# Layer 0 of a chain of attention layers: first-layer points in interleaved pairs, units folded over eight steps, one third-layer call per tile of scores

## The chip, the cores and the metric
The kernel runs on one core of a Trainium2 chip. The metric is the device time of one execution in microseconds (us). Smaller is better. All arithmetic is 32-bit floating point.

## The reference, cut to what matters
The program is a chain of four attention layers on an input of 2 x 512 channels x 32 x 32 pixels. The change lies in the first of them (layer 0), a deformable attention with 8 heads of 64 channels. Each head attends from 1,024 query pixels to 64 sampled key points. To the scores a bias is added that a small perceptron computes from the distance between query and key:

```python
pos = grid_q[:, :, None, :] - grid_kv[:, None, :, :]          # 1024 queries x 64 keys x (x, y)
bias = jnp.sign(pos) * jnp.log1p(jnp.abs(pos))
bias = jax.nn.relu(bias @ cpb_w1 + cpb_b1)                    # 2 -> 128
bias = jax.nn.relu(bias @ cpb_w2 + cpb_b2)                    # 128 -> 128
bias = (bias @ cpb_w3 + cpb_b3)                               # 128 -> 1
sim = jnp.einsum('bhid,bhjd->bhij', qh, kh) + bias
attn = jax.nn.softmax(sim, axis=-1)
```

There are 2 x 8 x 64 = 1,024 key points, and for each of them the perceptron runs on 1,024 queries. An output projection and a residual follow, then the feed-forward part of layer 0 and three further layers of attention, which the change does not touch.

## The kernel before
Layer 0 works through 8 tiles of scores (`NT`); a tile holds two heads, 128 key points by 1,024 queries. A tile has 32 steps (`NR`), each of four points. One long loop (line 892) runs over the 256 steps. The engines execute their instructions in the order in which the program issues them (`in_order`, line 58), so what is written into the loop first also stands first in the queue of each engine.

In each step:

- **First layer** (`first`, line 589, on VectorE). The logarithm of the distance separates into x and y, so a point's first layer is a table of 32 x-values (`tx`) plus a table of 32 y-values (`ty`), added and clipped at zero in one custom instruction (line 599) that writes 128 x 1,024 numbers `h1` (hidden units on the partitions, queries along the row). Four instructions a step, `AHEAD` = 7 points ahead of their use, into a ring of 11 buffers, 8 of them in the weight area `wa`. The tables for 16 points are loaded by SyncE's queue (`load_tabs`, line 573) and scaled by ScalarE (`scale_tab`, line 587) once in four steps.
- **Second layer** (`second`, line 609, on TensorE). The 128 outputs are computed in four parts of 32. For a part, the four points of the step use the four 32-column strips of the array side by side: 8 matmuls in the program, 16 records in the trace, into a PSUM tile `z` (three buffers of two banks). ScalarE applies bias and relu (line 625) into an SBUF tile.
- **Joining** (`joined`, line 630, on VectorE). The third layer's weights were moved into the second layer, up to a sign. Two instructions a step add part 0 to part 1 and part 2 to part 3. GpSimd's DMA then adds the second pair to the first (line 934, 512 KB, a DMA that accumulates in its destination). What is left is a *unit*: 4 points x 32 partial sums on the partitions.
- **Folding** (POOL's queue, accumulating DMAs). A unit's partitions are added in halves: odd onto even (line 927, 256 KB), then every second of those onto the first (128 KB). Four units in a row share one buffer, the *whole*: the first folds in itself (line 929), the other three copy half of what is left into the whole by SyncE (line 931) and add the other half by GpSimd (line 937).
- **Third layer** (`third`, line 635, on TensorE). Every 16 steps, four wholes are summed over their partitions by 8 matmuls with weights of +-1 and 0 into the tile of scores `sim` (one PSUM buffer). It happens 20 steps after the first unit of the 16 was begun (`due = i - 20`, line 899). The second call of a tile is followed by `scores` (line 653), and `sim` is then finished by a generator `behind`, which issues the rest of the tile's work in small pieces, two a step: `finish` (softmax; it holds `pt`, line 668, and `mx`, line 671), `offsets` (the 36 taps of a small convolution, line 408) and `samples` (the sampled keys; `pk` and `pvo`).

The wholes rotate through six buffers (`h2p`: `bridge` 0 to 5) and the other units through four (`h2j`). The last 16 steps (from `LAST`) go by twos in place of fours.

Of the kernel before, what the change touches and what calls it, by code (L numbers as in the profile page):

```python
# [19 lines left out]
P = 128  # L20
# [59 lines left out]
def kernel(ctx: ExitStack, tc: tile.TileContext, a: dict, out: bass.AP):  # L80
# [111 lines left out]
    def layer0(l0, fold_d, t2_b, o2_b):  # L192
# [6 lines left out]
        h2q = l0.enter_context(tc.tile_pool(name="att_h2q", bufs=3))  # L199
        h2p = cycle([bridge[:, k, :] for k in range(6)])  # L200
        h2j = cycle([bridge[:, 6, :], bridge[:, 7, :], *(one.tile([P, HW], F32, name=f"h2j{k}") for k in range(2))])
# [18 lines left out]
        qkw = next(h2j).rearrange("p (j q n) -> p j q n", j=2, q=NPAIR)  # L220
# [15 lines left out]
        ring = [one.tile([P, HW], F32, name=f"h1{k}") for k in range(3)]  # L236
        ring += [qkv2.rearrange("p k n -> p (k n)")[:, k * HW : (k + 1) * HW] for k in range(6)]
        ring += [proj2.rearrange("p k n -> p (k n)")[:, k * HW : (k + 1) * HW] for k in range(2)]
# [13 lines left out]
        ones = one.tile([P, P], F32, name="ones")  # L252
        nc.gpsimd.memset(ones, 1.0)
# [25 lines left out]
        w3_16 = one.tile([P, 48], F32, name="w3_16")  # L279
# [7 lines left out]
        def bias_weights():  # L287
            sort = h2b.tile([P, 7, P], F32, name="sort", tag="h2")
            row, below, w2t = [sort[:, k, :] for k in range(3)]
            perm = sort[:, 3:, :].rearrange("p b (r u) -> p b r u", u=32)  # L290
            few = one.tile([P, 28], F32, name="few")
# [69 lines left out]
            quarter = few[:, 26:28]  # L361
            for k in range(2):
                nc.vector.tensor_reduce(quarter[:, k : k + 1], ident[:, 2 + k : P : 4], AX.X, ALU.add)
                nc.vector.scalar_tensor_tensor(eighth, quarter[:, k : k + 1], 8.0, eighth, ALU.mult, ALU.add)
            nc.vector.tensor_scalar(w3_16[:, 16:32], row[:, 0:16], eighth, 0.0, ALU.add, ALU.is_equal)
            nc.vector.tensor_scalar(w3_16[:, 16:32], w3_16[:, 16:32], w3sign[:, 1:2], None, ALU.mult)
# [118 lines left out]
        def samples(t):  # L485
# [5 lines left out]
            ow = one.tile([P, C], F32, name="ow")  # L491
            nc.sync.dma_start(out=ow, in_=a["out_w"][pr * P : (pr + 1) * P, :])
# [18 lines left out]
            wx = one.tile([P, P], F32, name="wx")  # L511
# [15 lines left out]
            accumulate(pk[:, 1, :], [(wsum[:, 2:3].to_broadcast([P, P]), ident)])  # L527
            yield
            shift = one.tile([P, P], F32, name="shift")
# [12 lines left out]
            kq = one.tile([P, P], F32, name="kq")  # L542
# [3 lines left out]
            values = one.tile([P, P], F32, name="values")  # L546
# [12 lines left out]
        NCH = NR // 4  # L559
        LAST = NT * NR - 16  # L560
        tabs_of = {}

        def load_tabs(c):

            t, rc = divmod(c, NCH)
            assert t in tables
            tabs_of[c] = []
            for ax in range(2):
                src = slog_d[t, ax].rearrange("(q r) i -> q r i", q=4)
                tab = two.tile([P, 16, 32], F32, name=f"tab{ax}")  # L570
                if 4 * c < LAST:
                    q, r = rc % 4, rc // 4 * 16
                    nc.sync.dma_start(out=tab, in_=src[q, r : r + 16, :].partition_broadcast(P))
                else:
                    q, r = rc % 2 * 2, 16 + (rc - 4) // 2 * 8
                    nc.sync.dma_start(
                        out=tab.rearrange("p (q r) i -> p q r i", q=2),
                        in_=src[q : q + 2, r : r + 8, :].partition_broadcast(P),
                    )
                tabs_of[c].append(tab)  # L580

        def scale_tab(c, ax):
            tab, w = tabs_of[c][ax], col("cpb_w1", ax)
            if c == 0:
                nc.vector.tensor_scalar(tab, tab, w, 0.0 if ax else col("cpb_b1"), ALU.mult, ALU.add)
            else:
                nc.scalar.activation(tab, tab, AF.Identity, bias=0.0 if ax else col("cpb_b1"), scale=w)

        def first(p):

            chunk, point = divmod(p, 16)
            if point == 0:
                tabs_of.pop(chunk - 1, None)
                if chunk + 1 < NT * NCH:
                    load_tabs(chunk + 1)
            tx, ty = tabs_of[chunk]
            h1 = ring[p % len(ring)]

            nc.vector._custom_dve(  # L599
                TENSOR_ADD_SAT,  # L600
                out=h1.rearrange("p (y x) -> p y x", x=W),
                in0=tx[:, point, :].unsqueeze(1).to_broadcast([P, H, W]),
                in1=ty[:, point, :].unsqueeze(2).to_broadcast([P, H, W]),
                s0=float(np.finfo(np.float32).max),
                s1=0.0,
            )
            return h1

        def second(i, h1s, part):

            z = zt([P, HW], "z")
            lo = BLOCK[part]
            for half in range(2):
                n = slice(half * HALF, (half + 1) * HALF)
                for point in range(4):
                    nc.tensor.matmul(  # L616
                        z[point * 32 : point * 32 + 32, n],
                        cpb_w2[:, lo : lo + 32],
                        h1s[point][:, n],
                        start=True,  # L620
                        stop=True,
                    )
            ring = h2q if part % 2 else h2b if part else h2j if i % (4 if i < LAST else 2) else h2p
            h2 = ring.tile([P, HW], F32, name="h2", tag="h2") if ring in (h2q, h2b) else next(ring)
            nc.scalar.activation(h2, z, AF.Relu, bias=b2h[:, part : part + 1])  # L625
            return h2
# [8 lines left out]
        def third(sim, r, h2s, fours=(), halves=range(2), wide=False):  # L635

            for half in halves:
                n = slice(half * HALF, (half + 1) * HALF)
                w = w3_16[:, 16 - r : 48 - r] if wide else w3[:, 24 - r : 56 - r]
                ways = [(quad, w, h2) for quad, h2 in enumerate(h2s)]  # L640
                for k in range(2):
                    w = w3_4[:, 28 - r - 4 * k : 60 - r - 4 * k]
                    ways += [(quad, w, pair[k]) for quad, pair in enumerate(fours, len(h2s))]
                for k, (quad, w, h2) in enumerate(ways):
                    nc.tensor.matmul(
                        sim[quad * 32 : quad * 32 + 32, n], w, h2[:, n], start=(r == 0 and k < 4), stop=False
                    )
# [9 lines left out]
        def finish(t, sim):  # L657
# [4 lines left out]
            simb = one.tile([P, HW], F32, name="simb", tag="simb")  # L662
# [11 lines left out]
            at = one.tile([P, 8, P], F32, name="at", tag="simb")  # L674
# [42 lines left out]
        def finish_last(sim, eights, fours, right_sums, left_sums):  # L717
# [7 lines left out]
            simb = one.tile([P, HW], F32, name="simb", tag="simb")  # L725
# [90 lines left out]
        nat = [[next(h2p).rearrange("p (k n) -> p k n", k=2) for _ in range(2)] for _ in range(3)]  # L816
# [68 lines left out]
        h1s, parts, joins, sim, w1s = {}, {}, {}, None, None  # L885
        behind = chain(small_steps, offsets(1), samples(0))
        AHEAD = 7

        for p in range(AHEAD):
            h1s[p] = first(p)  # L890
        late_loads()
        for i in range(steps):
            for k, part in enumerate((1, 0, 3, 2)):
# [3 lines left out]
                if p < 4 * steps:  # L897
                    h1s[p] = first(p)
                due = i - 20
                if k == 1 and 0 <= due < LAST and due % 16 == 0:  # L900
                    t, r = divmod(due, NR)
                    if r == 0:
                        sim = ps_s.tile([P, HW], F32, name="sim")
                    third(sim, r, [joins.pop(due + j) for j in range(0, 16, 4)], wide=True)
                    if r:
# [10 lines left out]
                if LAST <= i - 2 and i < steps - 2:  # L916
# [4 lines left out]
                    if i - 3 >= LAST and i % 2 and k == 3:  # L921
                        nc.gpsimd.dma_start(out=joins[i - 3][1:P:2], in_=joins.pop(i - 2)[1:P:2], accum_op=ALU.add)
                if 0 <= i - 2 < LAST:
                    j = (i - 2) % 4
                    whole, own = joins[i - 2 - j], joins[i - 2]
                    if k == 0:
                        nc.gpsimd.dma_start(out=own[0:P:2], in_=own[1:P:2], accum_op=ALU.add)  # L927
                    if k == 3 and j == 0:
                        nc.gpsimd.dma_start(out=own[0:P:4], in_=own[2:P:4], accum_op=ALU.add)
                    if k == 3 and j:  # L930
                        nc.sync.dma_start(out=whole[j:P:4], in_=own[0:P:4])
                if k == 1 and i - 1 in parts:
                    other = joined(parts.pop(i - 1), 2)
                    nc.gpsimd.dma_start(out=joins[i - 1], in_=other, accum_op=ALU.add)  # L934
                j = (i - 3) % 4
                if k == 1 and 0 <= i - 3 < LAST and j:
                    nc.gpsimd.dma_start(  # L937
                        out=joins[i - 3 - j][j:P:4], in_=joins.pop(i - 3)[2:P:4], accum_op=ALU.add
                    )
# [5 lines left out]
                if k == 1 and due == LAST:  # L945
                    third(sim, 16, [joins.pop(due + j) for j in range(0, 8, 2)])
# [1325 lines left out]
```

## Time and profile before
| | |
|---|---|
| three runs | 3,348.35, 3,349.49, 3,349.53 us; median 3,349.49 |
| profiled execution | 3,353.46 us, span 3,351.7 us |
| mean granted TensorE clock | 0.998 of full speed |
| busy: TensorE, VectorE, ScalarE, GpSimd | 3,323.8, 2,673.0, 1,805.5, 676.7 us |
| first and last `z` matmul | 59.6 and 1,981.6 us |
| GpSimd's DMA queue | 68,400 packets, 231.26 MB |
| HBM read, written | 71.46 MB, 10.83 MB |

The profile names the engines PE (TensorE matmul), PEld (its weight loads), DVE (VectorE), ACT (ScalarE), POOL (GpSimd) and SP (SyncE). A group is named by line, engine, operation, and the tiles that it writes and reads. `wa` and `h` as outputs of line 599 are buffers of the ring `h1`; `bridge` and `h2j` are buffers of units. A wait is put down to what ended it.

### The profile page before, as it was taken

The numbers are of one execution on the slowest core, as the hardware profiler recorded it, in microseconds if no ns is written. First come the engines' busy times: TensorE is split into PE (matmuls) and PEld (weight loads), VectorE is DVE, ScalarE is ACT, GpSimd is POOL, SyncE is SP. The second block draws the span as 40 slices with busy tenths as digits, with TensorE's granted clock in tenths as the row PEclk, the third lists the DMA queues.
The fourth block names the chain that finished last, engine by engine and source line by source line (L and its number), as shares of the span: only waits on it lengthen the run. The fifth ranks groups of instructions, "written<-read, shape, count | busy, mean of one in ns | idle before, by whom it ended". The sixth has DMA issues, their size and how long they took to land.

```text
span 3351.7 us, 61808 instructions
## 1 busy us (share of the span) xinstructions
PE 3323.8 (99%) x24813; PEld 1611.7 (48%) x24813; DVE 2673.0 (80%) x3540; ACT 1805.5 (54%) x2774; POOL 676.7 (20%) x804
## 2 busy tenths in 40 slices
PE   9999999999999999999999999999999999999999
PEld 4333333332333332333333339999953443687777
DVE  6999999999999799999999976455446465665556
ACT  4866877877877577877877652122136245122221
POOL 0333333333333233333333310000000000000000
PEclk9999999999999999999999999999999999999999
DMA  5778787787787577787787751000100000000111
GB/s 166 157 161 166 153 168 156 152 166 153 158 167 155 103 162 155 159 169 152 158 166 157 161 135 58 14 8 14 52 0 14 26 29 20 7 7 3 30 32 36
DMA packets 142488, 343.97 MB, mean 103 GB/s; under 512 B 36464, under 2 KB 51440, under 8 KB 141424
## 3 DMA queue, kind: packets, MB, share of 16 engines
q0 software_dynamic: 68400, 231.26, 36.5%
q1 hardware_dynamic: 72496, 103.95, 10.7%
q8 instruction: 197, 3.23, 0.4%
q10 hardware_dynamic: 1296, 4.72, 0.4%
q14 instruction: 99, 0.81, 0.1%
HBM read 71.46 MB, written 10.83 MB: 25 GB/s over the span
## 4 chain that ended last, share of the span: by engine, by line
PE 82%; DVE 9%; issue 5%; DMA 2%; ACT 1%; POOL 1%; DVEq 0%; SPq 0%; POOLq 0%; ACTq 0%
PE z L616 38%; PE pma L135 6%; PE pw L1435 6%; PE pmb L135 5%; PE pmv L1435 4%; PE score L1614 3%; PE pv L1626 3%; DVE wa L599 3%; PE pm L1435 3%; PE score L1435 3%; PE pmt L1435 1%; PE ppr L1435 1%; DVE h L599 1%; DMA bridge<-h 1%; DVE bridge L630 1%
## 5 line engine op out<-in xcount | busy, mean ns | idle before, releaser
L616 PE MATMUL z<-wa,cpb_w 128*32 128x512 f32 x11904 | 1779.2, 593 | 5.8 <-ACT h L625 3.7
L625 ACT ACTIVATE h<-z,b2h 128x1024 f32<-128x1024 f32 x768 | 851.3, 1114 | 347.9 <-PE z L616 310.6
L616 PE MATMUL z<-h,cpb_w 128*32 128x512 f32 x4480 | 983.2, 593 | 1.6 <-ACT h L625 1.6
L616 PEld LDWEIGHTS z<-wa,cpb_w 128*32 128x32 f32 x11904 | 497.2, 110 | 888.2 <-issue 778.1
L599 DVE CUSTOM_DVE_ANT_1 wa<-tab,tab 128x1024 f32<-128x1024 f32 x744 | 878.1, 1216 | 1.3 <-PE z L616 1.1
L616 PEld LDWEIGHTS z<-h,cpb_w 128*32 128x32 f32 x4480 | 256.6, 110 | 328.6 <-issue 292.1
L599 DVE CUSTOM_DVE_ANT_1 h<-tab,tab 128x1024 f32<-128x1024 f32 x280 | 332.9, 1216 | 2.3 <-PE z L616 2.2
L630 DVE SCALAR_TENSOR_TENSOR h<-h,turn,h 128x1024 f32<-128x1024 f32 x256 | 326.8, 1276 | 4.3 <-ACT h L625 4.3
L625 ACT ACTIVATE bridge<-z,b2h 128x1024 f32<-128x1024 f32 x162 | 180.8, 1116 | 121.4 <-PE z L616 119.0
L927 POOL DMA_DIRECT2D bridge<-bridge x150 | 127.6, 850 | 547.2 <-DMA bridge<-h 510.5
L630 DVE SCALAR_TENSOR_TENSOR bridge<-bridge,turn,h 128x1024 f32<-128x1024 f32 x162 | 206.8, 1277 | 4.2 <-ACT bridge L625 4.2
L934 POOL DMA_DIRECT2D bridge<-h x161 | 163.4, 1015 | 213.2 <-DVE h L630 123.6
L1278 ACT COPY p<-pma 128x128 f32<-128x128 f32 x80 | 21.3, 266 | 334.7 <-PE pma L135 334.7
L1270 DVE TENSOR_TENSOR upper<-pma,p 128x256 f32<-128x256 f32 x80 | 33.7, 422 | 178.6 <-ACT p L1278 178.5
L1615 ACT ACTIVATE p<-score 128x512 f32<-128x512 f32 x256 | 130.0, 624 | 81.2 <-PE score L1614 79.6
L927 POOL DMA_DIRECT2D h2j<-h2j x90 | 76.2, 847 | 323.0 <-DMA h2j<-h 293.6
L1647 DVE TENSOR_TENSOR acc<-acc,p 128x1024 f32<-128x1024 f32 x96 | 111.0, 1217 | 19.4 <-ACT p L1615 19.3
L625 ACT ACTIVATE h2j<-z,b2h 128x1024 f32<-128x1024 f32 x94 | 105.0, 1117 | 37.9 <-PE z L616 37.3
L1614 PE MATMUL score<-q,k 64*128 64x512 f32 x512 | 120.7, 604 | 1.1 <-DVE gm L1191 1.1
L630 DVE SCALAR_TENSOR_TENSOR h2j<-h2j,turn,h 128x1024 f32<-128x1024 f32 x94 | 120.0, 1276 | 0.0
L1626 PE MATMUL pv<-p,vT 128*64 128x512 f32 x512 | 116.5, 598 | 0.0
L937 POOL DMA_DIRECT2D bridge<-h2j x90 | 111.9, 1244 | 2.6 <-issue 1.8
(458 smaller groups left out, 4379.8 us busy)
## 6 DMA issues: line engine op xcount, KB each, us to landing
bridge<-h POOLq DMA_DIRECT2D x161, 512.0 KB, 5.5
h2j<-h POOLq DMA_DIRECT2D x94, 512.0 KB, 5.9
bridge<-bridge POOLq DMA_DIRECT2D x159, 256.0 KB, 3.9
tab<-slog_d SPq DMA_DIRECT2D x128, 256.0 KB, 4.6
h2j<-h2j POOLq DMA_DIRECT2D x90, 256.0 KB, 3.2
bridge<-bridge POOLq DMA_DIRECT2D x150, 128.0 KB, 5.4
bridge<-bridge SPq DMA_DIRECT2D x90, 128.0 KB, 3.7
bridge<-h2j SPq DMA_DIRECT2D x90, 128.0 KB, 3.6
```

The source lines that it names most:

```text
L135: nc.tensor.matmul(pm, w, m, start=(k == 0), stop=(k == len(pairs) - 1))
L599: nc.vector._custom_dve(TENSOR_ADD_SAT, out=h1.rearrange("p (y x) -> p y x", x=W), in0=tx[:, point, :].unsqueeze(1).to_broadcast([P, H, W] ...
L616: nc.tensor.matmul(z[point * 32 : point * 32 + 32, n], cpb_w2[:, lo : lo + 32], h1s[point][:, n], start=True, stop=True,)
L625: nc.scalar.activation(h2, z, AF.Relu, bias=b2h[:, part : part + 1])
L630: nc.vector.scalar_tensor_tensor(h2, h2, turn[:, part // 2 : part // 2 + 1], parts.pop(part + 1), ALU.mult, ALU.add)
L927: nc.gpsimd.dma_start(out=own[0:P:2], in_=own[1:P:2], accum_op=ALU.add)
L934: nc.gpsimd.dma_start(out=joins[i - 1], in_=other, accum_op=ALU.add)
L937: nc.gpsimd.dma_start(out=joins[i - 3 - j][j:P:4], in_=joins.pop(i - 3)[2:P:4], accum_op=ALU.add)
L1435: nc.tensor.matmul(out, stationary(l, k), moving(r, k), start=start and k == 0, stop=k == nk - 1, skip_group_check=not start,)
L1614: nc.tensor.matmul(sc, ks[m][r, s * P : (s + 1) * P], qs[m][r, n], start=True, stop=True)
L1615: nc.scalar.activation(p[:, part], sc, AF.Exp, scale=64 ** -0.5)
L1626: nc.tensor.matmul(pv[half][part * 64 : part * 64 + 64], vt[s % 4][:, lo : lo + 64], lps[s, half][:, part, :], start=(s == 0), stop=(s == 7),)
```

## The change
First layer: two points per instruction. The ring holds six double buffers in which the 32-pixel rows of two points alternate. The table `ty` is written by ScalarE in the order (y, point), as `pairs`, so that (y, point) is one axis; the table loaded for it has one buffer instead of two. `second` reads each point with its rows 64 numbers apart. `AHEAD` is 8.

Folding: in the first seven tiles (`WIDE`) eight units share a whole. Every unit folds twice in itself, and a third time (64 KB) one step later: the first within itself, the others by a copy of 16 partitions and an accumulate of 16 partitions into the whole. The first half of the last tile keeps fours (`shared`), its last 16 steps twos.

Third layer: in the first seven tiles one call per tile with weights `w3_32`, 37 steps after the tile's first unit was begun.

Buffers: units and wholes take their buffers from one list of ten, `room`, in the order in which they come free. Parts 1 and 3 have four buffers instead of three. To make space, `ones` moves into a scratch tile, and `simb`, `at`, `wx`, `shift`, `kq`, `values` and `ow` share buffers with others; `ow` is loaded after `pk`.

```diff
-        h2q = l0.enter_context(tc.tile_pool(name="att_h2q", bufs=3))
-        h2p = cycle([bridge[:, k, :] for k in range(6)])
-        h2j = cycle([bridge[:, 6, :], bridge[:, 7, :], *(one.tile([P, HW], F32, name=f"h2j{k}") for k in range(2))])
+        h2q = l0.enter_context(tc.tile_pool(name="att_h2q", bufs=4))
+        room = deque([bridge[:, 7, :], *(one.tile([P, HW], F32, name=f"h2j{k}") for k in range(2))])
+        room += [bridge[:, k, :] for k in range(7)]
...
-        ring = [one.tile([P, HW], F32, name=f"h1{k}") for k in range(3)]
-        ring += [qkv2.rearrange("p k n -> p (k n)")[:, k * HW : (k + 1) * HW] for k in range(6)]
-        ring += [proj2.rearrange("p k n -> p (k n)")[:, k * HW : (k + 1) * HW] for k in range(2)]
+        ring = [one.tile([P, 2 * HW], F32, name=f"h1{k}") for k in range(2)]
+        ring += [qkv2.rearrange("p k n -> p (k n)")[:, k * 2 * HW : (k + 1) * 2 * HW] for k in range(3)]
+        ring.append(proj2.rearrange("p k n -> p (k n)"))
...
+        WIDE = (NT - 1) * NR
         LAST = NT * NR - 16
+
+        def shared(i):
+            return 8 if i < WIDE else 4 if i < LAST else 2
...
-                tab = two.tile([P, 16, 32], F32, name=f"tab{ax}")
+                tab = (one if ax else two).tile([P, 16, 32], F32, name=f"tab{ax}")
...
             tab, w = tabs_of[c][ax], col("cpb_w1", ax)
+            to = tab
+            if ax:
+                tab = tab.rearrange("p (a k) i -> p a i k", k=2)
+                to = two.tile([P, 8, 32, 2], F32, name="pairs")
+                tabs_of[c][ax] = to
...
-                nc.scalar.activation(tab, tab, AF.Identity, bias=0.0 if ax else col("cpb_b1"), scale=w)
+                nc.scalar.activation(to, tab, AF.Identity, bias=0.0 if ax else col("cpb_b1"), scale=w)
...
-            tx, ty = tabs_of[chunk]
-            h1 = ring[p % len(ring)]
+            tx, ty = tabs_of[chunk][0][:, point : point + 2, :], tabs_of[chunk][1][:, point // 2]
+            h1 = ring[p // 2 % len(ring)].rearrange("p (y k x) -> p y k x", k=2, x=W)
...
-                in0=tx[:, point, :].unsqueeze(1).to_broadcast([P, H, W]),
-                in1=ty[:, point, :].unsqueeze(2).to_broadcast([P, H, W]),
+                in0=tx.unsqueeze(1).to_broadcast([P, H, 2, W]),
+                in1=ty.unsqueeze(3).to_broadcast([P, H, 2, W]),
...
-            return h1
+            return [h1[:, :, k, :] for k in range(2)]
...
-                        h1s[point][:, n],
+                        h1s[point][:, half * 16 : half * 16 + 16, :],
...
-                due = i - 20
-                if k == 1 and 0 <= due < LAST and due % 16 == 0:
-                    t, r = divmod(due, NR)
-                    if r == 0:
-                        sim = ps_s.tile([P, HW], F32, name="sim")
-                    third(sim, r, [joins.pop(due + j) for j in range(0, 16, 4)], wide=True)
-                    if r:
+                for due, n in ((i - 37, 8), (i - 20, 4)):
+                    if k != 1 or not 0 <= due < LAST or due % NR or shared(due) != n:
+                        continue
+                    t = due // NR
+                    sim = ps_s.tile([P, HW], F32, name="sim")
+                    third(sim, 0, [taken(due + j) for j in range(0, 4 * n, n)], wide=w3_32 if n == 8 else w3_16)
+                    if n == 8:
...
                 if 0 <= i - 2 < LAST:
-                    j = (i - 2) % 4
-                    whole, own = joins[i - 2 - j], joins[i - 2]
+                    own, n = joins[i - 2], shared(i - 2)
+                    whole, j = joins[i - 2 - (i - 2) % n], (i - 2) % n
                     if k == 0:
                         nc.gpsimd.dma_start(out=own[0:P:2], in_=own[1:P:2], accum_op=ALU.add)
-                    if k == 3 and j == 0:
+                    if k == 3 and (n == 8 or j == 0):
                         nc.gpsimd.dma_start(out=own[0:P:4], in_=own[2:P:4], accum_op=ALU.add)
-                    if k == 3 and j:
+                    elif k == 3:
                         nc.sync.dma_start(out=whole[j:P:4], in_=own[0:P:4])
+                if k == 2 and 0 <= i - 3 < WIDE:
+                    own, j = joins[i - 3], (i - 3) % 8
+                    if j:
+                        nc.sync.dma_start(out=joins[i - 3 - j][j:P:8], in_=own[0:P:8])
+                    else:
+                        nc.gpsimd.dma_start(out=own[0:P:8], in_=own[4:P:8], accum_op=ALU.add)
...
-                j = (i - 3) % 4
-                if k == 1 and 0 <= i - 3 < LAST and j:
-                    nc.gpsimd.dma_start(
-                        out=joins[i - 3 - j][j:P:4], in_=joins.pop(i - 3)[2:P:4], accum_op=ALU.add
-                    )
+                for at in (i - 4, i - 3):
+                    if k != 1 or at < 0 or at >= LAST or (shared(at) == 8) != (at == i - 4):
+                        continue
+                    n = shared(at)
+                    j = at % n
+                    if j:
+                        own = taken(at)
+                        nc.gpsimd.dma_start(
+                            out=joins[at - j][j:P:n], in_=own[n // 2 : P : n], accum_op=ALU.add
+                        )
```

`taken(i)` removes unit `i` from the live units and puts its buffer at the end of `room`; part 0 of each step takes the buffer at the front.

## The prediction
> **What bounds the kernel now.** I read the page's busy shares and slices first, then the busy time by stretch, the costliest groups, the timelines of weight loads and of VectorE in a quiet stretch, and the waits.
>
> The page: TensorE (PE) 99%, VectorE (DVE) 80%.
> ```profile
> PE 3323.8 (99%) x24813; PEld 1611.7 (48%) x24813; DVE 2673.0 (80%) x3540; ACT 1805.5 (54%) x2774; POOL 676.7 (20%) x804
> DVE  6999999999999799999999976455446465665556
> ```
> The slices show that DVE's 80% is an average of two stages: nearly full until about 2,000 us (layer 0, which the change is in), half empty after. The busy time in four stretches of layer 0's loop says the same in us (columns: PE, PEld, DVE, ACT, POOL, clock, DMA share, GB/s):
> ```profile
> 60.00:500.00 440.00, 437.27 (x3976) 136.99 (x3972) 431.60 (x395) 331.74 (x444) 150.84 (x175) 1.00 0.78 163
> 500.00:1000.00 500.00, 496.57 (x4488) 156.06 (x4484) 487.56 (x445) 374.78 (x514) 175.26 (x204) 1.00 0.78 158
> ```
> PE and DVE are both full, the DMA engines are at 0.78. Two full engines cannot both set the pace, so the groups are asked:
> ```profile
> L616 PE MATMUL z<-wa,cpb_w 128*32 128x512 f32 x11904 | 1779.2, 593 | 5.8 <-ACT h L625 3.7
> L599 DVE CUSTOM_DVE_ANT_1 wa<-tab,tab 128x1024 f32<-128x1024 f32 x744 | 878.1, 1216 | 1.3 <-PE z L616 1.1
> L616 PE MATMUL z<-h,cpb_w 128*32 128x512 f32 x4480 | 983.2, 593 | 1.6 <-ACT h L625 1.6
> L630 DVE SCALAR_TENSOR_TENSOR bridge<-bridge,turn,h 128x1024 f32<-128x1024 f32 x162 | 206.8, 1277 | 4.2 <-ACT bridge L625 4.2
> ```
> The last column is idle time before the group: almost none on either engine. The 593 ns of a z matmul is a modelled end, so the pitch is taken from the weight loads (start, busy, engine, group, idle before):
> ```profile
> 623.38 0.13 PEld L616 LDWEIGHTS z<-wa,cpb_w 128*32 128x32 f32 x4 [0.30 <-issue]
> 623.81 0.13 PEld L616 LDWEIGHTS z<-wa,cpb_w 128*32 128x32 f32 x4 [0.30 <-issue]
> ```
> Four records start together, the next four 0.43 us later (0.4295 as a mean). The rows show 11,904 + 4,480 = 16,384 records, 4,096 fours, 16 in each of the 256 steps: 16 x 0.4295 = 6.87 us of PE a step, 1,759 us in all. From the first z (59.6) to the last (1,981.6) are 1,922 us. I laid all matmul starts of that stretch in order and subtracted each kind's usual pitch: what is left over is 33 us, 20 of it small pauses of about 0.1 us where the kind of matmul changes, and only 13 us in pauses over 0.25 us. **PE is 99% occupied by work that it must do.** DVE against that:
> ```profile
> 1000.81 2.35 DVE L599 CUSTOM_DVE_ANT_1 wa<-tab,tab 128x1024 f32<-128x1024 f32 x2
> 1003.08 1.28 DVE L630 SCALAR_TENSOR_TENSOR h<-h,turn,h 128x1024 f32<-128x1024 f32 x1
> 1004.28 2.35 DVE L599 CUSTOM_DVE_ANT_1 h<-tab,tab 128x1024 f32<-128x1024 f32 x2
> ```
> Two L599 and one L630 take 3.47 us by their starts (1000.81 to 1004.28), so DVE needs 6.93 us a step plus small work. It is a close second. Its waits tell that it is ahead of PE once a tile of 32 steps, when it meets work that comes late in PE's order (60 to 1,985 us; total, times, longest):
> ```profile
> DVE mx L671 <- PE pt L668: 29.4, 7, 5.8
> DVE x L715 <- PE pp L705: 23.1, 4, 7.1
> ```
> That is 52 us in which DVE had nothing to do.
>
> [...] the L599 pair starts 1,134 ns apart[...] The trace's 128 KB accumulates of L929 landed in 3.5 us[...]
>
> **The change part by part.**
> Third layer (PE): one call is 8 matmuls, 16 records, 4 fours: 1.72 us. The first seven tiles make one call instead of two: 7 x 1.72 = 12.0 us, all on PE, which is the path. **-12.0.** The eighth tile keeps its calls.
> First layer (DVE): 1,024 instructions of 1,134 ns become 512 of 2 x 1,067 + 67 = 2,200 ns: 34 us less on DVE, 6.80 a step, now under PE's 6.87. Off the path: 0. It can help only in the 13 us of pauses; I count -1.
> z's moving rows now jump every 32 elements. The trace has one such case, L343 in rows of 32 out of 128: its second pass was followed 0.112 us later by the next matmul, as contiguous ones of 128 columns are (`pk`, 0.112). 0[...].
> `scale_tab` (ScalarE, ACT): 63 of the 126 calls of 760 ns read with a stride. L408, strided, takes 408 ns for 64 elements and L678, contiguous, 313: 1.5 ns per element, so +0.75 us for 512. Once in four steps; in the busiest stretch (the 36 taps) ACT is busy 36.1 of 38.8 us, one or two such calls fit the 2.7 idle, and PE can run on in the other two of three z buffers (3.4 us). 0 to +4; I take +1.
> Folding (POOL and SP): each of the 224 wide steps issues one more GpSimd accumulate (16 rows, 64 KB), and the copy of SP shrinks from 32 rows to 16 but comes in 7 of 8 steps instead of 3 of 4. POOL's own loop: L927 is issued, 0.6 us later L934 (512 KB), whose landing the next L927 waits for.
> ```profile
> POOL bridge L927 <- DMA bridge<-h: 331.2, 94, 7.7
> POOL h2j L927 <- DMA h2j<-h: 200.0, 57, 6.3
> ```
> (of 400 to 1,600 us.) 0.6 + landing + 0.3 comes to 6.4 us, 7.7 in every fourth step where the tables load too, 6.8 as a mean; the step takes 7.50. The extra issue (0.83 to 1.25 us, L929 and L937) goes into the 3.4 us that POOL waits in each step; its data, 16 packets of about 0.29 us over 16 engines, adds 0.3 us of DMA time. The loop becomes about 7.1: still covered, no longer by much. What waits behind POOL: L934's source (3 buffers) and the room of part 0. By the order of the list of free buffers, freed units used to come back after two or three steps, now after three to five in most steps and after two in seven steps of a tile. I take +1, bounds -2 and the rival's price.
> The third call stands two steps behind the last fold, as before; PE's waits for it come to 1.5 us in all. With one stage more: 0.
> Edits with one answer: bias weights get about ten small DVE operations, 0.16 to 0.23 us each, 2 us, hidden in DVE's wait for `pb`:
> ```profile
> DVE o_b L855 <- PE pb L135: 8.0, 1, 8.0
> ```
> If that cover were gone, +2. Shared tags and the later `ow` load (SP waits for `pk`, with the next copies behind it) lie steps ahead of their users: 0. `AHEAD` 8 in pairs: two pairs (4.4 us) from 52.8 are ready at 57.2, before the first z: 0.
> **Sum**: -12.0 - 1 + 1 + 1 = -11. The profiled execution took 3,353.5 (span 3,351.7 and 1.8 around it), so it becomes 3,342.5; it was 4.0 above the median 3,349.5, which becomes **3,338.5**, rounded to 3,338.
>
> **The rivals.**
> (a) Forecast: PE's path, 3,332 to 3,342. Chance 0.57.
> (b) DVE does set the pace, and PE only looks full: for it the chain between 66 and 175 us, which runs through L599 and L630; against it the matmul starts. It would give 34 us, but PE's floor allows only 12 + 13: 3,325. Chance 0.06.
> (c) The saving comes back as waits: the later fold lands late at the third call (1.5 us x 7), or ACT's longer `scale_tab` meets the finish of a tile, which is one step later. 3,343 to 3,354. Chance 0.19.
> (d) Slower: POOL's loop becomes the bound. The extra accumulate doesn't hide, because the 256 KB one lands late (5.5 us in table steps) and the next L927 stands behind. It decides from a mean loop of 7.5 us. With half an issue and the data, 7.7: 224 x 0.2 = +45, 3,394; with a full one, 8.0: +112. For it: the chain at 118 to 162 us goes through POOL and `DMA bridge<-h`, and a pause of 1.8 us on PE follows at 175. Chance 0.12.
> (e) The strided rows slow z, up to 3,405. Chance 0.06. That the change doesn't do what it says is excluded by the instruction lists: 56 third-layer matmuls fewer, 512 L599-type instructions, 224 accumulates more.
>
> **How the numbers follow.** 0.2% (6.7 us) is about what a measurement can tell from no change. Faster: (a) and (b), 0.63; same: (c), 0.19; slower: (d) and (e), 0.18. The range leaves out (b)'s end and most of (d) and (e): 3,328 to 3,358; (a)'s own is 3,332 to 3,342.
>
> **What would show it.** Right: fours of z still 0.43 apart; sim's matmuls fewer, the loop's end 11 us earlier; DVE's share of the loop down from 96% (1,849 of 1,922 us) to about 94%, its waits on PE longer; the first-layer instruction near 2,200 ns by starts. Wrong: ACT's z evictions waiting for DMA, POOL without any wait for DVE (d), a z pitch over 0.43 (e), L599 above 2,300.

## The result, and the profile after

| | before | after |
|---|---|---|
| median, us | 3,349.5 (6 runs, 3,347.9 to 3,352.4) | 3,378.7 (6 runs, 3,375.1 to 3,384.1) |
| profiled span, us | 3,351.7 | 3,378.4 |
| mean granted TensorE clock, profiled execution | 0.998 | 0.997 |
| first and last `z` matmul, us | 59.6 and 1,981.6 | 59.8 and 2,005.1 |

The ratio is 1.009, 95% interval 1.0079 to 1.0100. The change is slower by 29 us, where 11 us faster were forecast. The z matmuls keep their pitch, about 0.43 us from one group of four to the next, so neither the clock nor the strided rows account for the loss (weight loads of the changed kernel):

```profile
623.34 0.13 PEld L635 LDWEIGHTS z<-h,cpb_w 128*32 128x32 f32 x4 [0.30 <-issue]
623.76 0.13 PEld L635 LDWEIGHTS z<-h,cpb_w 128*32 128x32 f32 x4 [0.30 <-issue]
```

The page of the changed kernel, first the busy shares and VectorE's slices:

```profile
PE 3322.3 (98%) x24701; PEld 1601.7 (47%) x24701; DVE 2642.3 (78%) x3039; ACT 1803.6 (53%) x2774; POOL 858.4 (25%) x1027
...
DVE  6998998998998798998998976464446566665656
```

PE has 112 records fewer (7 calls of 16). DVE's row now dips every third slice, once per tile. The stretches of the loop (columns as before):

```profile
60.00:500.00 440.00, 431.87 (x3908) 132.70 (x3900) 420.89 (x272) 328.45 (x438) 190.49 (x224) 1.00 0.84 162
500.00:1000.00 500.00, 491.96 (x4415) 151.89 (x4412) 475.61 (x309) 371.31 (x514) 229.63 (x270) 1.00 0.85 161
```

PE stood still for 8.1 and 8.0 us of them, against 2.7 and 3.4 before, though it had less to do. The waits of PE in the loop (what waits and what ended it; total, times, longest) name the place. The first line is from before, where L645 was the third-layer call; the others are from after:

```profile
PE sim L645 <- DMA bridge<-bridge: 1.5, 2, 1.3
...
PE sim L664 <- DMA bridge<-bridge: 15.6, 5, 3.9
PE z L635 <- ACT h2j L644: 6.1, 3, 3.0
PE sim L664 <- DMA h2j<-h2j: 3.9, 1, 3.9
...
PE sim L664 <- DMA bridge<-h2j: 3.1, 1, 3.1
PE sim L664 <- DMA bridge<-h: 2.9, 1, 2.9
```

L664 is the third-layer call; it waits once in each of the first seven tiles, and at the end of the eighth in `finish_last`. In the line of L635 and `h2j` PE waits for ScalarE's part 0, and ScalarE, by its own waits, for a buffer of `room`, which a late accumulate still reads or fills:

```profile
ACT bridge L644 <- DMA bridge<-bridge: 28.5, 15, 3.7
ACT h2j L644 <- DMA bridge<-h2j: 12.0, 3, 5.8
```

In all ScalarE waits 61 us for DMAs in the loop, which is one of the signs of being wrong that the prediction named; the other, POOL without any wait for DVE, did not appear. The forecast added nothing to the 1.5 us of waits at the third-layer call and +1 for the room of part 0. Repeating the sum of PE's starts over the loop, pauses within the third-layer call come to 28.6 us (2.0 before), pauses between z matmuls to 18.9 (6.9 before): +26.6 and +12.0 against the 12.0 saved. That is the 26.7 us by which the span of the profiled execution grew; 23.4 of them lie before the last z, the rest at the call in `finish_last`.

**One of these waits, read in order.** Around the second tile's call, from the timeline of all engines (start, length, engine and line, idle before):

```profile
326.55 0.85 POOL L951 DMA_DIRECT2D bridge<-bridge  x1 [2.11 <-DMA bridge<-h]
...
327.09 1.22 POOL L964 DMA_DIRECT2D bridge<-h  x1
...
327.66 1.46 POOL L972 DMA_DIRECT2D bridge<-h2j  x1
...
329.94 1.03 PE L664 MATMUL sim<-bridge,w 128*32 128x512 f32 x6
...
330.46 0.84 POOL L953 DMA_DIRECT2D bridge<-bridge  x1 [0.57 <-DMA bridge<-bridge]
...
334.45 0.85 POOL L951 DMA_DIRECT2D bridge<-bridge  x1 [3.16 <-DMA bridge<-h]
...
334.83 1.88 PE L664 MATMUL sim<-bridge,w 128*32 128x512 f32 x10 [3.85 <-DMA bridge<-bridge]
```

POOL issues a unit's 512 KB accumulate (L964) and the last 64 KB one of an older unit (L972), waits for the 256 KB fold to land and issues L953, and waits for the 512 KB to land and issues L951. From one L951 to the next are 7.9 us. PE begins the call at 329.94, is through six records and stands 3.85 us, until this L972, which brings in the tile's last unit, has landed (at 334.48 by its DMA record).

**The loop.** I took the steps in which POOL issued the 512 KB accumulate (L934 before, L964 after) straight after the first fold (L927, L951), so that nothing but landings set its pace, and measured from one first fold to the next. This period, *the loop*, is 0.85 us of issue plus the landing of the 512 KB accumulate ("tables" are steps in which the first layer's tables load, "fold" is the 128 KB one of L929 or L953 beside it):

| | steps | loop without tables, us | with tables and fold, us | mean, us | 512 KB lands after (no tables), us |
|---|---|---|---|---|---|
| before | 105 | 6.59 | 8.13 | 6.86 | 5.74 |
| after | 171 | 7.16 | 8.54 | 7.50 | 6.31 |

PE's step is 6.87 us of z. Before, POOL's loop just kept up. Now it does not. Call *lag* the distance from the start of ScalarE's part 0 to the L964 of the same step, as the median over the tiles for each place in the tile (single steps reach more). The lag, 2 to 5 us before in most steps, grows within each tile to 7 to 8.5 us, and falls to 1 us where PE stands at the call. At the call 7 to 8 of lag, 0.6 of issues ahead and 6 to 7 of landing make some 15 us. The order of the loop leaves two steps, 13.7 us, less the 1.7 that the part's own z matmuls take between the call and ScalarE: 12.0. About 3 are missing, and 2.7 to 4.1 are what PE stood at the seven calls.

The chain that ended last shows it in one line, by engine (before it was 82% PE and 2% DMA), and by line:

```profile
PE 55%; DMA 30%; issue 6%; DVE 5%; POOL 4%; ACT 1%; DVEq 0%; POOLq 0%; SPq 0%; ACTq 0%
DMA bridge<-h 21%; PE z L635 13%; DMA h2j<-h 6%; PE pma L135 6%; PE pw L1470 6%; PE pmb L135 5%; PE pmv L1470 4%; PE score L1649 3%; PE pv L1661 3%; PE pm L1470 3%; PE score L1470 3%; DMA bridge<-bridge 2%; POOL bridge L951 2%; PE ppr L1470 1%; DVE wa L618 1%
```

### The profile page after: what moved, and what is told of

The parts are those of the page before. It is cut to its first block, busy times and chain, and to the rows that moved or that the text cites. A ratio compares the mean times of both kernels' runs of the same rounds, so it can differ in the third digit from the quotient of the medians.

```text
span 3378.4 us, 61170 instructions
## 1 busy us (share of the span) xinstructions
PE 3322.3 (98%) x24701; PEld 1601.7 (47%) x24701; DVE 2642.3 (78%) x3039; ACT 1803.6 (53%) x2774; POOL 858.4 (25%) x1027
## 2 busy tenths in 40 slices
DMA packets 147859, 349.44 MB, mean 103 GB/s; under 512 B 40496, under 2 KB 55472, under 8 KB 146800
## 4 chain that ended last, share of the span: by engine, by line
PE 55%; DMA 30%; issue 6%; DVE 5%; POOL 4%; ACT 1%; DVEq 0%; POOLq 0%; SPq 0%; ACTq 0%
DMA bridge<-h 21%; PE z L635 13%; DMA h2j<-h 6%; PE pma L135 6%; PE pw L1470 6%; PE pmb L135 5%; PE pmv L1470 4%; PE score L1649 3%; PE pv L1661 3%; PE pm L1470 3%; PE score L1470 3%; DMA bridge<-bridge 2%; POOL bridge L951 2%; PE ppr L1470 1%; DVE wa L618 1%
## 5 line engine op out<-in xcount | busy, mean ns | idle before, releaser
L635 PE MATMUL z<-wa,cpb_w 128*32 128x512 f32 x10880 | 1195.2, 593 | 8.6 <-ACT h2j L644 6.1
L618 DVE CUSTOM_DVE_ANT_1 wa<-tab,pairs 128x2048 f32<-128x2048 f32 x340 | 776.4, 2284 | 5.0 <-PE z L635 4.7
L635 PEld LDWEIGHTS z<-wa,cpb_w 128*32 128x32 f32 x10880 | 346.2, 110 | 819.1 <-issue 707.5
L635 PE MATMUL z<-h,cpb_w 128*32 128x512 f32 x5504 | 609.4, 593 | 3.2 <-ACT h L644 1.7
L618 DVE CUSTOM_DVE_ANT_1 h<-tab,pairs 128x2048 f32<-128x2048 f32 x172 | 392.8, 2284 | 2.7 <-PE z L635 2.6
L635 PEld LDWEIGHTS z<-h,cpb_w 128*32 128x32 f32 x5504 | 174.5, 110 | 413.3 <-issue 351.7
L951 POOL DMA_DIRECT2D bridge<-bridge x184 | 156.1, 849 | 502.4 <-DMA bridge<-h 482.4
L649 DVE SCALAR_TENSOR_TENSOR bridge<-bridge,turn,h 128x1024 f32<-128x1024 f32 x197 | 251.8, 1278 | 8.1 <-ACT bridge L644 7.8
L964 POOL DMA_DIRECT2D bridge<-h x196 | 216.9, 1107 | 139.9 <-DVE h L649 126.6
L953 POOL DMA_DIRECT2D bridge<-bridge x174 | 153.4, 882 | 227.7 <-DMA bridge<-bridge 215.7
L972 POOL DMA_DIRECT2D bridge<-bridge x141 | 190.7, 1353 | 2.1 <-issue 2.1
L644 ACT ACTIVATE h2j<-z,b2h 128x1024 f32<-128x1024 f32 x59 | 65.9, 1117 | 72.4 <-PE z L635 48.1
```

What stands on the lines that cost most here:

```text
L618: nc.vector._custom_dve(TENSOR_ADD_SAT, out=h1, in0=tx.unsqueeze(1).to_broadcast([P, H, 2, W]), in1=ty.unsqueeze(3).to_broadcast([P, H, 2, ...
L635: nc.tensor.matmul(z[point * 32 : point * 32 + 32, n], cpb_w2[:, lo : lo + 32], h1s[point][:, half * 16 : half * 16 + 16, :], start=True, ...
L649: nc.vector.scalar_tensor_tensor(h2, h2, turn[:, part // 2 : part // 2 + 1], parts.pop(part + 1), ALU.mult, ALU.add)
L972: nc.gpsimd.dma_start(out=joins[at - j][j:P:n], in_=own[n // 2 : P : n], accum_op=ALU.add)
```

## The experiments

Each is told against the kernel before, measured beside it (median 3,350.4 or 3,350.5 us); a ratio is to that. Theory 1 blames POOL's queue, theory 2 only the place of the third-layer call, theory 3 the pairs. Later theory 1 is split: 1a says that the work of the extra accumulates makes the queue late, 1b that POOL does by waiting, in order, for transfers that it issued only just before.

**Pairs with the folding of before.** In the changed kernel, fours, two calls a tile and three buffers of parts 1 and 3 are put back:

```diff
-        WIDE = (NT - 1) * NR
+        WIDE = 0
...
-                for due, n in ((i - 37, 8), (i - 20, 4)):
+                for due in (i - 20,):
```

> The change with its folding undone: pairs in the first layer, but four units per whole, two third-layer calls per tile and three buffers for parts 1 and 3, as before. Theory 1 (POOL's loop: the one accumulate more per step makes GpSimd's queue slower than a step of pure z matmuls, folds fall behind within a tile, the third-layer call and part 0 of later units wait): no extra accumulate, so 3,340 to 3,350 us, PE's waits for folds as before (about 2 us in all). Theory 2 (only the place of the third-layer call, two steps after the last fold, is too early for a chain with one stage more): the same, 3,340 to 3,350. Theory 3 (the pairs cost: strided z rows, the strided scaling of the table, coarser DVE instructions): above 3,360, most of the loss still there.

Measured: 3,344.3 us (3,341.4 to 3,347.2), ratio 0.998 (0.9973 to 0.9988). The pairs, with the new list of buffers and the shared ones, are 6 us faster, so in sum neither they nor the strided rows cost anything. Their stretch of z matmuls is 1,910 us against 1,922 before. By PE's starts, about 5 of these 12 us lie in the third-layer calls, 4 between z matmuls, and 3 at the first z after `po`, the matmul behind the taps: before, it started 0.77 us behind `po` in five of seven tiles, now 0.18 in all. That DVE is now ahead with the points is the likely reason; it was not tried by itself. About 5 us are given back after the last z: PE gets there earlier and waits in `finish_last` for the last folds (`pt` begins 15.4 us after the last z in place of 10.7).

**The fold without pairs**: the changed kernel with single points.

```diff
-            tx, ty = tabs_of[chunk][0][:, point : point + 2, :], tabs_of[chunk][1][:, point // 2]
+            tx, ty = tabs_of[chunk]
...
-                if p < 4 * steps and k % 2 == 0:
-                    h1s[p], h1s[p + 1] = first(p)
+                if p < 4 * steps:
+                    h1s[p] = first(p)
```

> The other half alone: first layer by single points as before, but eight units per whole and one third-layer call per tile. Theory 1: 3,374 to 3,390, as slow as the change or a few us slower, since joins come no earlier. Theory 2: the same. Theory 3: below 3,350, since 12 us of PE are saved and no pairs are there.

Measured: 3,379.8 us, ratio 1.0091 (1.0076 to 1.0106). The whole loss is in the folding with its later call and its buffers; theory 3 is out.

**The call one step later**, one buffer moved from parts 1 and 3 to `room` for it:

```diff
-        h2q = l0.enter_context(tc.tile_pool(name="att_h2q", bufs=4))
+        h2q = l0.enter_context(tc.tile_pool(name="att_h2q", bufs=3))
...
-                for due, n in ((i - 37, 8), (i - 20, 4)):
+                for due, n in ((i - 38, 8), (i - 20, 4)):
```

> The change with the third-layer call of the seven wide tiles one step later (38 steps after the tile's first unit, not 37), and one buffer moved from parts 1 and 3 to the list of unit buffers, so that part 0 has at least two steps behind a freed unit. Theory 2: PE's 25 us of waits at the third-layer calls vanish and nothing takes their place, 3,348 to 3,355. Theory 1: POOL is no longer set back at each call by PE's stall, its lag runs on, and a good part of the wait returns as ACT waiting for DMA and PE waiting for ACT: 3,356 to 3,374.

Measured: 3,358.4 us (3,351.4 to 3,369.5), ratio 1.0027 (1.0015 to 1.0039). The median lies in theory 1's band, near its edge. 20 of the 29 us are back. With three steps of slack PE hardly waits at the tiles' calls. The first wait of PE is now another, on work of POOL that has nothing to do with folding:

```profile
PE z L635 <- ACT qpad L399: 8.7, 4, 3.9
...
ACT qpad L399 <- POOL qpad L393: 12.8, 4, 5.0
```

`qpad`'s padding is cleared by POOL, behind the waiting accumulates in the same queue. The mean loop is still 7.40 us, the lag, a median over the tiles as above, reaches 9.4. Slack hides part of a queue that is late; the queue stays late.

**Without the last accumulate**: seven of eight units in the first seven tiles do not add their last 16 rows, so half of what they fold is left out.

```diff
-                        nc.gpsimd.dma_start(
...
+                        if n < 8:
+                            nc.gpsimd.dma_start(
```

> The change without the 16-row accumulate that ends the folding of seven units in eight (half of these units' folded sums is left out); all copies, the other three accumulates and the third-layer calls stay. Theory 1: POOL has as many issues per step as before and the saving on PE comes out: 3,334 to 3,345, lag of L964 behind ACT back to 2 to 5 us. Theory 2: the copies end the chain now and come earlier than the accumulate did, but the lag within a tile is unchanged: 3,345 to 3,360. Theory 3: above 3,365.

Measured: 3,339.1 us, ratio 0.9968 (0.9957 to 0.9979), the time that theory 1 gave, but not for its reason: POOL is still late (mean loop 7.32, lag 7 to about 10). What is gone is the last landing of the chain of folds: the units are complete once SP's copies land, and PE's waits at the tiles' calls are gone. The theory was incomplete: a late queue costs only through those who wait for it.

**The extra accumulate alone.** To the pairs with fours a free accumulate is added in each of 220 steps, 16 rows of a spare buffer onto themselves, for which nobody waits:

```diff
+                if k == 1 and 4 <= i < NT * NR - NR:
+                    nc.gpsimd.dma_start(out=spare[0:P:8], in_=spare[4:P:8], accum_op=ALU.add)
```

> Pairs with folding by fours (the first experiment, 3,344 us), plus one free GpSimd accumulate of 16 rows (64 KB) in each of 220 steps on a buffer that nobody else uses, issued behind L964. Theory 1a (what costs is one more issue and 64 KB more in POOL's queue): POOL's lag behind ACT grows to 7 us and more, 3,356 to 3,380. Theory 1b (POOL's loop runs over the landing of L964, and what lengthens that is the 32-row fold L953, which every step now issues while L964 is in flight): the free accumulate waits for nothing and stands behind L964, so 3,342 to 3,353.

Measured: 3,352.4 us, ratio 1.0007 (0.9999 to 1.0016), 8 us above the pairs with fours. This is in 1b's band and below 1a's. The mean loop goes from 6.69 to 7.07, and by PE's starts the time is lost at the third-layer calls. The work of one more small accumulate costs something, but not the 34 us between the pairs with fours and the change.

**A 32-row accumulate in each step**, in L953's place, waiting for L951 as L953 does:

```diff
                         nc.sync.dma_start(out=whole[j:P:4], in_=own[0:P:4])
+                        nc.gpsimd.dma_start(out=spare[0:P:4], in_=own[2:P:4], accum_op=ALU.add)
```

> Pairs with folding by fours, plus a 32-row accumulate (128 KB) in the place of L953 in the three of four steps that had none there: it reads the unit's own rows, so it waits for L951's landing as L953 does in the change, and adds them into a buffer that nobody reads. Theory 1b: landing of L964 from 5.4 up to 5.9 us or more, lag of L964 behind ACT up to 6 to 9 us, and the third-layer calls, which wait for an accumulate two steps old, stall PE: 3,355 to 3,380. Theory 1a: about the same as the free 16-row accumulate of the run beside it.

Measured: 3,346.8 us, ratio 0.9992 (0.9983 to 1.0000), 2.5 us above the pairs with fours; 1b had given at least 3,355, and 1a the time of the run before it, so both missed. A wait that ends before the 512 KB landing, for which POOL waits anyway, adds little (mean loop 6.92). So neither addition makes the loss by itself; the two together, with fours, were not tried.

**The same transfers, issued in another order.** The changed kernel with the later call and its buffer as above, and POOL's accumulates arranged so that what each works on was issued about a step earlier or more: the 512 KB accumulate of the youngest unit goes first, the folds follow one stage per step, the copy comes a step later and the last accumulate five steps behind.

```diff
-                    if k == 0:
+                    if k == 2:
                         nc.gpsimd.dma_start(out=own[0:P:2], in_=own[1:P:2], accum_op=ALU.add)
...
+                if k == 3 and 0 <= i - 3 < WIDE:
+                    own = joins[i - 3]
+                    nc.gpsimd.dma_start(out=own[0:P:4], in_=own[2:P:4], accum_op=ALU.add)
+                if k == 2 and 0 <= i - 4 < WIDE:
+                    own, j = joins[i - 4], (i - 4) % 8
...
-                for at in (i - 4, i - 3):
+                for at in (i - 5, i - 3):
```

> The change with POOL's order in a step altered: L964 of the youngest unit first, then the last accumulate of a unit five steps old, then the first fold (L951) of a unit two steps old, then the second fold (L953) of a unit three steps old; copy, last accumulate and third-layer call one step later (38), one buffer moved from parts 1 and 3 to the list. The same transfers, but no accumulate waits for one issued just before it. Theory 1b: POOL is not held by landings, its lag stays below 5 us, PE's pauses fall to about those of before and the 12 us come out: 3,330 to 3,342. Theory 1a: POOL has as many issues and bytes as in the change, lag and waits stay: 3,352 to 3,375.

Measured: 3,345.0 us (3,341.6 to 3,352.8), ratio 0.9985 (0.9979 to 0.9992): 34 us faster than the change with as many issues, packets (147,859) and bytes (349.44 MB on all queues). Against the later call alone (3,358.4), with the same buffers, the order is worth 13 us. That counts it low: the last accumulate comes a step later too, so the call again stands only two steps behind it, as in the change. With the slack at the call unchanged and no accumulate left out, the wait at the seven calls is gone. The lag, as a median over the tiles, is down to 5.5 us at most. The time lies between the bands, nearer to 1b's.

**The order alone, with fours.** Only L951 goes behind L964; the last accumulate (L972) keeps its place.

```diff
-                    if k == 0:
+                    if k == 2:
                         nc.gpsimd.dma_start(out=own[0:P:2], in_=own[1:P:2], accum_op=ALU.add)
```

> Pairs with folding by fours, only the first fold of a unit (L951) issued behind L964 of the next unit instead of ahead of it. Theory 1b: POOL's lag smaller than in the first experiment, time the same to 5 us lower, 3,338 to 3,345, since PE has few pauses left there. Theory 1a: no change from 3,344.

Measured: 3,547.9 us, ratio 1.0594 (1.0577 to 1.0611), far from anything expected. POOL's longest waits in the loop:

```profile
POOL bridge L972 <- DMA bridge<-bridge: 683.2, 117, 8.7
POOL bridge L972 <- DMA bridge<-h2j: 288.6, 53, 8.8
```

L972, three quarters of a step later, now waits in POOL's queue for SP's copy, which waits for the L951 just issued: two landings in a row stand in the loop, and L964 behind them. I had moved one issue and not its dependents. By these waits it is the same mechanism in a strong form: with the same transfers as the pairs with fours, the time is 204 us longer.

**The last wait removed.** In the reordered version PE still stood 4.6 us at the last tile's first call, whose fold had moved and the call not. One number is changed (the line with the minus is that of the reordered version):

```diff
-                for due, n in ((i - 38, 8), (i - 20, 4)):
+                for due, n in ((i - 38, 8), (i - 21, 4)):
```

> The piped version (e6_piped) with one number changed: in the last tile, which keeps units of four, the first third-layer call comes 21 steps after the tile's first unit in place of 20. In e6_piped PE stood 4.64 us at that call (at 1,877 us) plus some 1.6 us in small gaps just after it, because the fold of the 256 KB accumulate had been moved two quarters of a step later and the call had not. Theory (PE's floor plus its waits sets the time): those 5 to 6 us go, 3,338 to 3,342. Rival (the wait comes back at the next point where PE needs the folded units, in finish_last, where e6_piped already waited 3.47 us): 3,343 to 3,348, with the pause at the end grown to 6 us or more.

Measured: 3,337.7 us (3,335.9 to 3,338.5), ratio 0.996 (0.9946 to 0.9974): 12.7 us faster than before and 41 faster than the change, just under the band of its theory. The wait at the end did not grow. The waits of POOL and of PE in this version:

```profile
POOL bridge L967 <- DVE h L649: 520.4, 125, 43.7
POOL h2j L967 <- DVE h L649: 270.5, 66, 18.0
POOL bridge L975 <- DMA bridge<-bridge: 44.2, 15, 8.1
```
```profile
PE z L635 <- ACT h L644: 4.5, 10, 0.7
PE sim L664 <- DMA bridge<-h: 3.3, 1, 3.3
```

L967 is the 512 KB accumulate here, L975 the last one. POOL waits mostly for DVE, the producer; its waits for landings are some 180 us in all, against 930 in the change. Not all transfers are quicker for it: the 512 KB ones land sooner than in the change (5.3 us after issue, as a median, in place of 6.2), but the 256 KB folds later (6.1 in place of 3.6), and PE no longer waits for it in the first seven tiles.

```profile
bridge<-h POOLq DMA_DIRECT2D x176, 512.0 KB, 5.3
bridge<-bridge POOLq DMA_DIRECT2D x173, 256.0 KB, 6.1
```

The chain of this version is 95% PE:

```profile
PE 95%; DVE 1%; issue 1%; ACT 1%; DMA 1%; POOL 0%; SPq 0%; DVEq 0%; ACTq 0%; POOLq 0%
```

## Why the prediction was wrong

The step that failed is **"Folding … The loop becomes about 7.1: still covered"**, and with it **"The third call … With one stage more: 0"** and the +1 for part 0's room.

- **The loop.** The working took 6.8 as the mean loop and added 0.3 for data. The base was nearly right: 6.86 in the steps in which POOL had no slack, the only ones that say whether a loop can keep up. The addition was 0.64 in place of 0.3, because the landing of the 512 KB accumulate, for which POOL waits, itself grew (5.74 to 6.31 without tables) when more accumulates were under way beside it. The working charged only the data of the new one, at 0.29 us a packet; that is the mean of POOL's queue with its packets of a few bytes in it, and the packets of 4 KB took 0.34. The issue time was rightly put into POOL's waiting: in the loop of 7.16 there is still only one issue of 0.85.
- **The bound.** I compared the loop with a "step" of 7.50 us, the stretch divided by 256. PE's step outside the tile's end is 6.87 of z and little else. At the 7.1 of the forecast the loop would already have been late there. A mean over stages of different pace hid it, and rival (d)'s threshold of 7.5 was wrong for the same reason.
- **The third call.** "Two steps behind the last fold, as before" is right as a count of steps. But the 13.7 us now had to hold 8 us of lag: +26.6 us of PE's pauses. Rival (c) named this wait but priced it at 1.5 us a tile; it was 2.7 to 4.1. The +1 for part 0's room was the rest: +12.0 between z matmuls.
- **Rival (d)** named the mechanism: POOL's loop as the bound, L951 standing behind a landing. Its price, +45, counted a stall in every step; the loss is paid at the calls and at part 0, where buffers run out, and the slack was used up first.
- **Right.** Third layer -12.0: 56 matmuls fewer, z groups still 0.43 us apart. First layer: one instruction of two points takes 2.20 us by starts, the forecast to the hundredth. From start to next start the medians are 1,135 ns for a single point before and 2,202 ns for two after: the second 1,024 numbers took 1,067 ns, and 68 ns are left that an instruction costs once, as in the forecast's working:

```profile
998.62 2.28 DVE L618 CUSTOM_DVE_ANT_1 wa<-tab,pairs 128x2048 f32<-128x2048 f32 x1
1000.82 1.27 DVE L649 SCALAR_TENSOR_TENSOR bridge<-bridge,turn,h 128x1024 f32<-128x1024 f32 x1
```

  Rival (e), strided rows, is excluded by the pitch and by the pairs with fours; its price, up to 3,405, was a guess of the author's that no trace showed. The prelude cost hardly anything: the first z is at 59.8 (59.6).
- **Wrong but small.** `scale_tab` with stride: 844 ns against 810 for its contiguous neighbour, not +750. Pairs: -6 in all, not -1. Part of what single points cost PE was hidden by the working itself: subtracting each kind's usual pitch counted the 0.77 us from `po` to z as pitch, though 0.6 of it was a wait, 3 us in all.
- **Luck.** The reordered version gains 12.7 us, about the 11 forecast, but not by the forecast's sum. From the pairs with fours to it the third-layer calls shrink by the 12.0, yet some 5 us come back between z matmuls, so that the wide folding is worth 6.6; the pairs bring the other 6. Two errors cancel. It does show that the idea can pay; the order of POOL's queue, with the calls placed too close behind it, took the gain away.
- **Open.** How the loop's +0.64 divides between the 32-row fold in each step and the 16-row one was not settled: leaving the latter out gives 7.32 from 7.50; added alone to the version with fours it brings 0.38, and the 32-row one 0.23. Nor is it settled how much of the change's loss the later call and the extra buffer would each recover, as the two were only moved together.

## What to carry to other kernels

An engine that issues DMAs in order and waits for landings is a loop of its own (here 7.50 us against the 6.87 of PE's step): find its period in the steps in which it has no slack, and set it against the pace of the stage it serves, not against a mean over stages. Before adding a transfer to such a queue, arrange the queue so that each entry depends only on what was issued about a step earlier, youngest producer first; then, as here, more stages cost latency and buffers more than time (3,345.0 us with the wide folding reordered, 3,344.3 with fours). When one entry is moved, move all that depends on it (L951 moved alone cost 204 us), and the reader at the end too (its move brought 3,345.0 to 3,337.7).

## What the runs showed of the hardware

Small accumulating DMAs were slow in company. The prediction charged the new 64 KB accumulate 0.3 us of DMA time, worked out from its packets; in the changed kernel the 64 KB accumulates landed 6.1 us after issue (median), about as late as the 512 KB ones (6.2):

```profile
bridge<-h POOLq DMA_DIRECT2D x196, 512.0 KB, 6.2
...
bridge<-bridge POOLq DMA_DIRECT2D x159, 64.0 KB, 6.1
```

Nearly all of them are issued about 0.6 us behind a 512 KB one. The kernel before showed it already: its 128 KB accumulates of L929 landed after 3.5 us, but those of the same size of L937, which were issued behind a 512 KB one as the new ones are, after 5.9 (medians of all; the line has the half that read `h2j`):

```profile
bridge<-h2j POOLq DMA_DIRECT2D x90, 128.0 KB, 5.7
```

In these runs the landing depended on what was ahead more than on the size, so a price from size alone was far too low. And the DMA engines' mean share was no warning: 0.84 in the change, 0.86 in the fastest version.
